# Two rations of filler products for TensorE inside one step of a scan loop

## The chip, the core and the metric

The kernel runs on one core of one Trainium2 chip. A core has five engines that run side by side, each through its own queue: TensorE (PE in the profile, with its weight loads as PEld), VectorE (DVE), ScalarE (ACT), GpSimd (POOL) and SyncE (SP), which here only issues DMAs. The metric is device time in microseconds (us), the median of several runs; smaller is better.

## What is computed

Two layers are applied to an input `x` of 4 batches, 512 channels and 64 x 64 = 4096 positions, in float32. Cut to what matters:

```python
# layer 0: x = x + mamba_layer(group_norm(x)); the 512 channels are 4 chunks of 128
xn  = layer_norm(group_norm(x))
xz  = chunk @ in_proj_w.T                 # 2 x 256 columns: xi and z
xc  = silu(causal_conv4(xi))
dt, Bs, Cs = split(xc @ x_proj_w.T)       # 8, 16 and 16 columns
dt  = softplus(dt @ dt_proj_w.T + dt_proj_b)
h_t = exp(dt_t * A) * h_(t-1) + (dt_t * x_t) * B_t      # 256 x 16 states, 4096 times
y_t = sum_over_states(h_t * C_t) + xc * D
ym  = (y * silu(z)) @ out_proj_w.T + skip * chunk
x   = x + layer_norm(ym) @ proj_w.T + proj_b
# layer 1: x = x + linear_attention(group_norm(x)), 8 heads of 64
q, k = relu(x @ w_q.T), relu(x @ w_k.T)
kq   = k.T @ q, summed over all 4096 positions of a batch
out  = (v @ kq) / kq.sum() @ w_out.T + b_out
```

Layer 1 of a batch can only start when layer 0 of that batch is done, since its group norm and `kq` need all positions.

## The kernel before, in words

**Steps and slots.** Layer 0 is cut into 128 steps: 4 batches, 8 tiles of 512 positions each, 4 chunks of 128 channels (`steps`, in this order). A step is cut into `SLOTS` = 16 slots. A slot makes two scans of 128 x 512 (L741, DVE), the two decays `dA` that they read (L715, ACT, written to three PSUM banks, three scans ahead), and one product `bx` of 128 x 1024 (L723, POOL, two slots ahead). Every second slot closes four scans of one group of states: DVE multiplies them by `c_all` (L761), POOL their last quarter (L753), and TensorE sums over the states into `y` (`fold_states`, 16 short matmuls). So even slots hold one DVE operation more than odd ones.

**Work with a fixed slot.** The inner function `after()`, called at the end of each slot, also issues what the step needs at fixed places: `time_banks` in slot 2, the two softplus in slot 3, `out_proj` of the step before in slot 4, the convolution and gate inputs of the step after next (`front`: `pc`, `pz`) in slots 3 and 5 to 9, its `mixers` (`pd`) in slots 12 to 15 and 0, 1. `take_y` (L780) copies a finished `y` out of PSUM on ACT in slots 8 and 0.

**Filler.** All other work is written as generators that issue a little and then yield. They stand in four lists: `ahead` (the norm of the next tile), `late` (`leave`: the second layer norm, the projection `pp`, the residual add, the statistics of layer 1), `rest` (`attention` of a finished batch: `pq` and `pk`, then the small `pm`, `pob`, and the output `pr`) and `light` (statistics of the next batch). A piece of `pq`, `pp` or `pr` is two products; a bank is filled by two such pieces, with `yield "more"` between them.

**The credit.** `mm()` counts every matmul in units of one 128 x 512 float32 product: bf16 ones count a quarter, ones of which several run side by side a share. At the end of each slot the credit grows by a ration and shrinks by what the slot issued; it never exceeds 2.6. Then each list gets one turn: `ahead` always, `late` and `rest` only while the credit is positive (or for a piece that uses no TensorE, or for the second half of a bank if nothing large was issued in this turn). `limit` and `room` bound how many PSUM banks filler may hold (1 in slots 1 to 5, else 2), `later(n, ...)` puts an eviction `n` slots after its matmuls (`soon()`: 2 in slots 5 to 11, else 1), and `TILES` = 3 bounds the 1 MB tiles in SBUF.

```python
limit[0] = 1 if 0 < s < 6 else 2
credit = min(credit + 3.5 - (work["mm"] - seen), 2.6)
busy = False
for queue in (ahead, late, rest):
    kind = queue[0][1] if queue else None
    if queue is ahead or kind == "free" or credit > 0 or kind == "more" and not busy:
```

**The order is fixed at build time.** All of this is Python that runs when the program is built. On the chip each engine gets a fixed list of instructions; nothing is decided by time.

**After the last slot** what stands in the lists is issued without credit, banks or due times:

```python
add_to(late, leave(B - 1, NT - 1))
while late or rest:
    one(late) or one(rest)
```

The attention of the last batch can only be here, since its layer 0 ends with the last slot. `rest` is a first-in first-out list: an attention of an earlier batch that isn't finished comes first.

Of the kernel before, what the change touches and what calls it, by code (L numbers as in the profile page):

```python
# [24 lines left out]
def kernel(  # L25
# [100 lines left out]
    work = {"mm": 0.0}  # L126
# [486 lines left out]
    def time_banks(f, nm):  # L613

        f["pt"] = [work_bank(f"pt_{nm}_{e}", 0) for e in range(NH)]
        for e in range(NH):
            r = slice(e * LANE, (e + 1) * LANE)
            mm(f["pt"][e], w_dt[r, :], f["dtr"][r, :], start=True, stop=True, abreast=NH)

    def time_steps(f, nm):  # L620
        for e in range(NH):
            nc.scalar.activation(  # L622
                f["both"][:, 0, e, :], f["pt"][e], AF.Softplus, bias=dtb[:, e : e + 1]
            )

    def to_rows(f, v, nm):

        both = f["both"]
        if v:
            nc.gpsimd.tensor_tensor(f["both"][:, 1], f["both"][:, 0], f["xz"][:, 0], ALU.mult)  # L630
        d_rows = dram.tile([P, NH, T], F32, tag=f"d_rows{v}", name=f"d_rows{v}_{nm}")
        f["d_rows", v] = d_rows
        later(1, lambda: nc.sync.dma_start(d_rows, both[:, v]))

    def spread(f, e, nm, part):

        if part == 0:
            f["d_all", e] = wk.tile([P, 2, NJ, T], F32, tag="d_all", name=f"d_all_{nm}_{e}")
        v, half = divmod(part, 2)
        src = f["d_rows", v].rearrange("(j i) e t -> i e j t", i=BLK)[:, e]  # L640
        for k in range(half * KS // 2, (half + 1) * KS // 2):
            nc.sync.dma_start(f["d_all", e][k * BLK : (k + 1) * BLK, v], src)
# [136 lines left out]
    def take_y(f, n, e):  # L779
        nc.scalar.copy(f["xz"][:, 0, e, :], ys.pop((n, e)))  # L780

    def gate(f, e):
        nc.gpsimd.tensor_tensor(  # L783
            f["xz"][:, 1, e, :], f["xz"][:, 1, e, :], f["xz"][:, 0, e, :], ALU.mult
        )

    def out_proj(f, xn, c, nm):
        po = f["po"] = work_bank(f"po_{nm}", 0)
        diagonal(po, skd, xn[:, c, NTAP - 1 : NTAP - 1 + T])
        for e in range(NH):  # L790
            mm(po, w_op[:, e, :], f["xz"][:, 1, e, :], start=False, stop=(e == NH - 1))

    def with_skip(f, xn, c):
        nc.scalar.copy(xn[:, c, NTAP - 1 : NTAP - 1 + T], f["po"])
# [239 lines left out]
    def leave(b, t):  # L1034
        if t == 0:
            stats1[b] = shifted_stats(b)
            x1s[b] = [
                dram.tile([P, NC, T], F32, tag="x1", name=f"x1_{b}_{i}", bufs=3 * NT)
                for i in range(NT)
            ]  # L1040
        ym = xn[b, t][:, :, NTAP - 1 : NTAP - 1 + T]
        yield from projected(ym, stats1[b], x1s[b][t], b, t)
        if t == NT - 1:
            add_to(rest, attention(b, x1s[b], stats1[b]))
# [5 lines left out]
    def silu(n):  # L1050
        xz = fs[n]["xz"].rearrange("p i e t -> p (i e) t")
        nc.scalar.activation(xz[:, : 2 * NH - 1], xz[:, : 2 * NH - 1], AF.Silu)  # L1052
        nc.scalar.activation(xz[:, 2 * NH - 1], fs[n]["pz"], AF.Silu)
# [3 lines left out]
    def add_to(queue, pieces):  # L1057
        queue.append([pieces, None])
# [3 lines left out]
    def one(queue, may=ANYWHERE):  # L1062

        while queue:
            if queue[0][1] not in (None, "wait", "more", "free") and queue[0][1] not in may:
                return False
            queue[0][1] = next(queue[0][0], queue)
            if queue[0][1] is not queue:  # L1070
                return queue[0][1] != "wait"
            queue.pop(0)
        return False
# [26 lines left out]
    with tc.manual_schedule():  # L1100
        credit, seen, mix, held[0], held_x[0] = 0.0, work["mm"], iter(()), 0, 0
        for n, (b, t, c) in enumerate(steps):
# [10 lines left out]
            for s in range(SLOTS):  # L1113
                def after():
                    nonlocal credit, seen
                    now[0] = n * SLOTS + s
                    for what in [w for at, w in due if at <= now[0]]:
                        what()
                    due[:] = [d for d in due if d[0] > now[0]]
                    if s == 0 and before is not None:  # L1120
                        take_y(before, n - 1, 1)
                    if s == SLOTS // 2:
                        take_y(f, n, 0)
                    if s < 2:
                        next(last_mix, None)
                    if s < 4:
                        spread(f, 1, nm, s)
                    if s == 1 and before is not None:
                        gate(before, 1)
                    if s == 2 and nxt is not None:  # L1130
                        time_banks(nxt, names[n + 1])
                    if s == 3 and nxt is not None:
                        nc.scalar.preload_act_table_set("softplus")
                        time_steps(nxt, names[n + 1])
                        nc.scalar.preload_act_table_set("natural_log_exp_and_others")
                    if s == 6 and before is not None:
                        pb_, pt_, pc_ = steps[n - 1]
                        with_skip(before, xn[pb_, pt_], pc_)
                        if pc_ == NC - 1:
                            add_to(late, leave(pb_, pt_))  # L1140
                    if s in (3, 5, 6, 7, 8, 9):
                        next(front, None)
                    if s == 4 and nxt is not None:
                        to_rows(nxt, 0, names[n + 1])
                        to_rows(nxt, 1, names[n + 1])
                    if s == 4 and before is not None:
                        pb_, pt_, pc_ = steps[n - 1]
                        out_proj(before, xn[pb_, pt_], pc_, names[n - 1])
                    if s == 9:
                        gate(f, 0)  # L1150
                    if 8 <= s < 12 and nxt is not None:
                        spread(nxt, 0, names[n + 1], s - 8)
                    if s == 10 and n + 2 < N:
                        silu(n + 2)
                        nc.scalar.preload_act_table_set("natural_log_exp_and_others")
                    if s >= 12:
                        next(mix, None)
                    may = [
                        what for k, what in ((0, "wide"), (1, "one ahead"), (2, "two ahead"))
                        if any(a - 2 * k <= s <= a - k for a in AWAY) or (k == 2 and s == SLOTS - 1)  # L1160
                    ]
                    if light and light[0][1] == "wait" or s in AWAY and not any(
                        q and q[0][1] == "wide" for q in (ahead, late)
                    ):
                        one(light)

                    limit[0] = 1 if 0 < s < 6 else 2
                    credit = min(credit + 3.5 - (work["mm"] - seen), 2.6)
                    busy = False
                    for queue in (ahead, late, rest):  # L1170
                        kind = queue[0][1] if queue else None
                        if queue is ahead or kind == "free" or credit > 0 or kind == "more" and not busy:
                            start = work["mm"]
                            one(queue, ANYWHERE if queue is ahead and (c, s) > (1, 4) else may)
                            credit -= work["mm"] - start
                            busy = busy or work["mm"] - start > 1
                    seen = work["mm"]

                slot(n * SLOTS + s, N * SLOTS, after)
            fs[n - 1].clear() if n else None  # L1180
        product(N * SLOTS - 1)
# [64 lines left out]
```

## Time and profile before

| | |
|---|---|
| Median of 3 runs | 7841.29 us (7840.99 to 7841.53) |
| The profiled execution | 7841.65 us, span 7839.9 us |
| Busy in the span | DVE 88%, POOL 88%, PE 82%, ACT 70% |
| First and last scan start | 121.4 and 7362.8 us |
| After the last scan's end (7364.0 us) | 475.9 us |

The span runs from the first to the last instruction. The rest of the profiled execution's time, 1.75 us, lies around it. In the page "busy" is the time in which an engine works on something; for PE it is not a measure of its peak. The span has two parts that must be read apart: the scan loop from 121 to 7364 us, and a tail in which DVE and POOL have nothing to do. Inside the loop the 4096 scans of L741 are a clock: two are one slot, 32 are one step.

### The profile page before, as it was taken

How to read it: one execution, taken by the hardware profiler on the slowest of the kernel's cores; microseconds unless marked ns; L12 is line 12 of the kernel's file. 1: busy time of each engine (PE TensorE's matmuls, PEld its weight loads, DVE VectorE, ACT ScalarE, POOL GpSimd, SP SyncE). 2: the span in 40 equal slices, each digit the busy share in tenths (PEclk: the TensorE clock that was granted, in tenths of full speed). 3: DMA queues.
4: the chain of work that ended last, by engine and by line, in shares of the span. 5: the costliest groups of instructions: out<-in, count | busy, mean ns of one | idle time of the engine just before them, and what ended most of it. 6: DMA issues, size and time to landing. Idle time of an engine off the chain costs nothing.

```text
span 7839.9 us, 90362 instructions
## 1 busy us (share of the span) xinstructions
PE 6444.6 (82%) x24837; PEld 2113.0 (27%) x24880; DVE 6904.3 (88%) x5650; ACT 5457.0 (70%) x8329; POOL 6904.2 (88%) x4649
## 2 busy tenths in 40 slices
PE   5676777677788888898788888898788888988599
PEld 1121211111223222332222223332122232322144
DVE  5999999999999999999999999999999999999500
ACT  4667777777777777777777777777777777777421
POOL 4999999999999999999999999999999999999500
PEclk7788878888899999998899999999899999999799
DMA  5676666666666666776766666677666666577302
GB/s 163 164 172 165 160 152 162 158 161 166 173 171 171 154 168 166 183 192 172 178 161 173 172 165 162 169 188 181 165 162 167 160 167 156 146 211 182 98 33 91
DMA packets 829183, 1265.86 MB, mean 161 GB/s; under 512 B 183912, under 2 KB 317560, under 8 KB 816384
## 3 DMA queue, kind: packets, MB, share of 16 engines
q1 hardware_dynamic: 804736, 1222.32, 61.2%
q0 software_dynamic: 16896, 33.56, 2.5%
q10 hardware_dynamic: 7040, 4.20, 0.2%
q8 instruction: 195, 3.19, 0.2%
q14 instruction: 316, 2.59, 0.1%
HBM read 1052.78 MB, written 206.57 MB: 161 GB/s over the span
## 4 chain that ended last, share of the span: by engine, by line
DVE 33%; PE 31%; ACT 11%; DMA 8%; issue 7%; POOL 6%; SPq 3%; POOLq 0%; DVEq 0%; ACTq 0%
DVE h L741 21%; DVE h L761 10%; PE y L124 6%; PE pc L124 6%; PE pq L124 5%; POOL bx L723 4%; ACT dA L715 4%; DMA d_all<-d_rows 3%; PE pr L124 3%; PE po L124 3%; PE pp L124 2%; SPq L690 2%; DMA c_sb<-c_rows 2%; PE c_all L124 1%; DMA b_all<-b_rows 1%
## 5 line engine op out<-in xcount | busy, mean ns | idle before, releaser
L723 POOL TENSOR_TENSOR bx<-d_all,b_all 128x1024 f32<-128x1024 f32 x2048 | 4829.5, 2369 | 184.7 <-DVE h L741 164.6
L741 DVE TENSOR_TENSOR_SCAN h<-dA,st,bx 128x512 f32<-128x512 f32 x3584 | 4360.0, 1269 | 317.0 <-ACT dA L715 132.8
L715 ACT ACTIVATE dA<-d_all,a_t 128x512 f32<-128x512 f32 x4096 | 2758.2, 687 | 1491.7 <-DVE h L741 1435.2
L761 DVE TENSOR_TENSOR h<-h,c_all 128x1536 f32<-128x1536 f32 x1024 | 1772.4, 1731 | 0.1
L753 POOL TENSOR_TENSOR h<-h,c_sb 128x512 f32<-128x512 f32 x1024 | 1301.4, 1271 | 108.2 <-DMA c_sb<-c_rows 21.8
L124 PE MATMUL y<-h,fold 128*32 128x512 f32 x8192 | 1271.8, 697 | 30.9 <-POOL h L753 27.3
L124 PE MATMUL c_all<-parts,sel 128*128 128x384 bf16 x1024 | 368.4, 360 | 1077.4 <-DVE h L761 1075.7
L124 PE MATMUL pc<-xn,w_cv 128*128 128x512 f32 x2048 | 1045.0, 644 | 120.8 <-DVE xn L414 63.3
L124 PE MATMUL pq<-w_qk,xa 128*128 128x512 f32 x2048 | 967.8, 606 | 7.5 <-issue 5.0
L741 DVE TENSOR_TENSOR_SCAN h<-dA,bx 128x512 f32<-128x512 f32 x512 | 590.6, 1206 | 80.7 <-ACT dA L715 57.9
L124 PEld LDWEIGHTS <-sel 128*128 128x128 bf16 x1280 | 127.3, 100 | 1733.2 <-DVE h L761 1537.4
L124 PEld LDWEIGHTS pc<-xn,w_cv 128*128 128x128 f32 x2048 | 388.9, 201 | 740.7 <-issue 417.7
L124 PEld LDWEIGHTS pq<-w_qk,xa 128*128 128x128 f32 x2048 | 397.7, 196 | 446.8 <-issue 428.2
L124 PE MATMUL pr<-xb,m 128*128 128x512 f32 x1024 | 477.8, 605 | 5.5 <-ACT res L982 2.8
L124 PE MATMUL pp<-xn,w_pr 128*128 128x512 f32 x1024 | 478.0, 597 | 3.8 <-DVE xn L414 3.8
L124 PE MATMUL y<-xz,dg 32*32 32x512 f32 x2048 | 358.9, 778 | 0.0
L124 PEld LDWEIGHTS y<-h,fold 128*32 128x32 f32 x8192 | 170.5, 114 | 619.6 <-issue 377.1
L783 POOL TENSOR_TENSOR xz<-xz 128x512 f32<-128x512 f32 x256 | 325.9, 1273 | 8.9 <-ACT xz L780 8.3
L834 ACT ACTIVATE kq<-pq 128x512 f32<-128x512 f32 x256 | 150.6, 588 | 260.0 <-PE pq L124 259.0
L630 POOL TENSOR_TENSOR dt<-dt,xz 128x1024 f32<-128x1024 f32 x128 | 302.5, 2363 | 27.8 <-ACT dt L622 27.8
L124 PE MATMUL pd<-xz,w_xp 128*128 128x512 f32 x512 | 309.1, 734 | 5.2 <-ACT xz L1052 5.2
L124 PE MATMUL pz<-xn,w_z 128*128 128x512 f32 x512 | 273.2, 625 | 9.9 <-ACT xz L609 8.5
(178 smaller groups left out, 5927.6 us busy)
## 6 DMA issues: line engine op xcount, KB each, us to landing
d_all<-d_rows SPq DMA_DIRECT2D x2048, 256.0 KB, 4.4
b_all<-b_rows SPq DMA_DIRECT2D x4096, 64.0 KB, 2.4
d_rows<-dt SPq DMA_DIRECT2D x256, 512.0 KB, 3.0
c_sb<-c_rows SPq DMA_DIRECT2D x4096, 16.0 KB, 3.6
xs<-in_x_dram SPq DMA_DIRECT2D x32, 1024.0 KB, 7.5
xn<-in_x_dram SPq DMA_DIRECT2D x32, 1024.0 KB, 8.8
xr<-in_x_dram POOLq DMA_DIRECT2D x32, 1024.0 KB, 10.0
x<-xr SPq DMA_DIRECT2D x32, 1024.0 KB, 4.2
```

Of the source, the lines that this page charges most:

```text
L124: nc.tensor.matmul(out_, lhsT, rhs, **how)
L630: nc.gpsimd.tensor_tensor(f["both"][:, 1], f["both"][:, 0], f["xz"][:, 0], ALU.mult)
L690: nc.sync.dma_start(dst[k * BLK : (k + 1) * BLK, :], rows_[q * KS + k, :].partition_broadcast(BLK))
L715: nc.scalar.activation(dAs[k], fs[n]["d_all", e][:, 0, j, :], AF.Exp, scale=a_t[:, e, j, q : q + 1])
L723: nc.gpsimd.tensor_tensor(bxs[g], fs[n]["d_all", e][:, 1, jj * 2 : jj * 2 + 2, :], bc(b_all[g // JJ], 2), ALU.mult)
L741: nc.vector.tensor_tensor_scan(h[:, j, :], dAs.pop(2 * g + i), bxs[g][:, i, :], 0.0 if t == 0 else st[:, c, e, q, j : j + 1], ALU.mult, AL ...
L753: nc.gpsimd.tensor_tensor(h[:, :, CUT:], h[:, :, CUT:], bc(c_sb.pop(g // JJ), NJ), ALU.mult)
L761: nc.vector.tensor_tensor(own, own, bc(c_all.pop(g // JJ), NJ), ALU.mult)
L783: nc.gpsimd.tensor_tensor(f["xz"][:, 1, e, :], f["xz"][:, 1, e, :], f["xz"][:, 0, e, :], ALU.mult)
L834: nc.scalar.activation(qk[i], pq, AF.Relu)
```

## The change

One line of `after()` is different: the ration that a slot adds to the credit.

```diff
                     limit[0] = 1 if 0 < s < 6 else 2
-                    credit = min(credit + 3.5 - (work["mm"] - seen), 2.6)
+                    credit = min(credit + (2.5 if 2 <= s < 10 else 4.5) - (work["mm"] - seen), 2.6)
                     busy = False
                     for queue in (ahead, late, rest):
```

Slots 2 to 9 of each step add 2.5 products in place of 3.5, slots 10 to 15 and 0 and 1 add 4.5. The sum over a step is 56 both times, and the cap of 2.6 and everything else stay.

## The prediction, as put on record before the changed kernel ran

> **What bounds the kernel now.** I read the busy table and the 40 slices of the page first. DVE and POOL are at 9 tenths until slice 37 and then at 0 while PE is at 8 or 9: a loop in which DVE and POOL are full, and a tail that belongs to PE.
>
> ```profile
> PE 6444.6 (82%) x24837; PEld 2113.0 (27%) x24880; DVE 6904.3 (88%) x5650; ACT 5457.0 (70%) x8329; POOL 6904.2 (88%) x4649
> ...
> PE   5676777677788888898788888898788888988599
> ...
> DVE  5999999999999999999999999999999999999500
> ```
>
> Then sums by window, cut where the scan count says that eight steps end: two windows of eight steps without attention, then two with it, then the tail.
>
> ```profile
> 999.00:1441.00 442.00, 321.08 (x1188) 86.22 (x1188) 423.24 (x328) 322.67 (x491) 429.58 (x288) 0.81 0.66 158
> 1441.00:1883.00 442.00, 318.00 (x1188) 85.61 (x1188) 423.17 (x327) 322.90 (x491) 429.62 (x288) 0.82 0.66 158
> 2334.00:2795.00 461.00, 403.94 (x1670) 137.49 (x1673) 437.92 (x366) 345.67 (x534) 430.99 (x288) 0.95 0.67 170
> 2795.00:3255.00 460.00, 403.72 (x1656) 141.05 (x1657) 428.46 (x344) 342.74 (x528) 433.03 (x294) 0.93 0.65 161
> ```
>
> The columns are PE, PEld, DVE, ACT and POOL, busy us and count. A step takes 442 / 8 = 55.2 us without attention, of which POOL works 429.6 / 8 = 53.7: its floor. With attention it takes 57.6, POOL working 53.9. So attention costs some 2.4 us a step, nearly all of it waiting. Next the waits of DVE from 2334 to 3255 us (16 steps), and the chain of waits over the tail.
>
> ```profile
> DVE h L741 <- ACT dA L715: 16.2, 18, 3.4
> DVE h L741 <- PE y L124: 11.1, 11, 2.3
> DVE h L741 <- ACT kq L834: 8.3, 3, 3.0
> ```
>
> ```profile
> 7389.88 15.71 PE pp L124 x32
> ...
> 7673.26 7.40 PE pq L124 x18
> 7681.44 3.61 PE pq L124 x8
> 7685.78 0.71 PE pk L124 x16
> 7689.36 20.05 PE pm L124 x40
> 7709.41 11.23 PE pob L124 x64
> 7722.82 113.10 PE pr L124 x256
> ```
>
> In the loop late PE results stop ACT, and through it the decays and DVE. In the tail PE alone counts, and one attention stands there: its `pr` rows are 256 instructions, two for each of 8 x 4 x 4 = 128 products.
>
> **What the Trainium skill says.** "PSUM — Partial Sum Buffer", section Engine vs sequencer instructions: the queues of ScalarE, VectorE and GpSimd are strictly first-in first-out, and matmuls complete in program order. The trace agrees: DVE waited 8.3 us above for an eviction of `kq`, which has nothing to do with scans. "SBUF — State Buffer", section Who interferes with whom: a DVE operation with at most one SBUF input, outside the two-port modes, doesn't contend with GpSimd. The scan and L761 each have one operand in PSUM, and the scan's time is even here (1217 to 1297 ns), so moving filler shouldn't stretch DVE's or POOL's own operations. "Perfetto Trace Analysis", section Identifying the Most-Contended Engine: matmul busy time is a poor measure of how full TensorE is. I therefore count products.
>
> **The change, part by part.** No operation is added or removed; pieces move between slots, and possibly out of the loop. The credit rule is plain arithmetic on product counts, so where each piece falls can be counted from the code for both rations. Means per attention step (steps 40 to 59 before and after):
>
> - Slots 2 to 9, all products: 29.0 before, 22.3 after. Of `rest` 6.3 before, 1.2 after. Slots 4 to 9 alone, 21.6 to 15.8.
> - Slots 10 to 15, 0, 1: 21.8 before, 23.9 after. Of `rest` 10.1 before, 10.7 after.
> - Whole step: 50.8 before, 46.3 after.
>
> The sum of the rations is 56 both times, but a turn of `rest` issues one piece of about two products, and credit above 2.6 is lost. In slots 10 to 1 `rest` already ran nearly every turn, so 4.5 there buys little; the 2.5 in slots 2 to 9 is eaten by fixed work. Throughput of filler falls by about 4.6 products a step, and attention no longer keeps pace. Before, the attentions of batches 0, 1 and 2 end at step 62 slot 15, 94 slot 15 and 125 slot 9. After, the list is never empty from step 35 on, and at the loop's end 5734.3 - 5502.0 = 232.3 products of batch 2's attention are left.
>
> *The tail.* 232.3 is: 2 + 1 + 4.25 for what remains of the 24th of 32 position blocks, 8 x 9.5 for eight whole ones, 1 for the last `pk`, 4 + 16 for `pm`, 128 for `pr`, and `pob`, small in products. Their duration is read from the same pieces of batch 3 in the tail of before. A block starts every (7673.26 - 7440.84) / 29 = 8.014 us, and the last starts at 7676.85 (PE's rows in order of time); so the 25th starts at 7676.85 - 7 x 8.014 = 7620.8. `pr` ends at 7722.82 + 113.10 = 7835.9. That is 215.1 us. The rest of the 24th block is 7.25 products of 8.014 / 9.5 = 0.84 us: 6.1. Together 221.
>
> Can the backlog hide in a gap? PE stands idle today from the end of `pp` (7405.6) to the first full `pq` (7427.2), mostly for the residual DMA and statistics on ACT. The backlog can use some 6 us of it; the next block's norm is behind the statistics on ACT (done at 7421.9) and needs two evictions (0.6 each) and 0.8 more, so PE waits to about 7424. In exchange a new joint opens between the two attentions: the last eviction (0.7), the load of the first tile behind the last stores on SP (7.6 us to landing), and a norm of 0.8, some 10 us. These cancel to about +1. Tail: +222 us, bounds 210 and 232.
>
> *The loop.* Steps 35 to 127 take 7364.0 - 2045.2 = 5318.8 us before: 84 at about 57.6, 9 without attention at about 54.4. After, all 93 carry attention. By slot (two scans each), DVE's idle time a step in steps 36 to 61 is 0.73 us in slot 5, 0.28 in 6, 1.07 in 8, 0.19 in 10; in steps 4 to 34 it is 0.39, 0.01, 0.29, 0.01. PE is hardly idle from slot 5 to 9 and still has the 5.5 products of slot 4 before it. With 15.8 products in slots 4 to 9, fewer than the 18.2 of steps 4 to 29, I expect these four slots to fall to the smaller values: -1.5. Against it, slots 12 to 15 go from 12.0 to 13.4 products, with evictions one slot later; their length is 4.24 + 2.66 + 4.03 + 2.53 = 13.5 us, and at 0.84 the 13.4 fill 11.3 of it. A heavy slot 12 (5.1) may delay ACT and `take_y` in slot 0. No row shows this; it lies between 0 and the 1.1 by which the early slots suffered. I take +0.3. A step then takes 57.6 - 1.5 + 0.3 = 56.4 us; 93 x 56.4 = 5245, so -74. Bounds: 55.6 (only POOL's floor and the old idle) gives -148, 57.0 gives -18. Steps 0 to 34 hold the same 34 products a step in the stretch 4 to 29, only later in the step, and stand at 55.2 against POOL's 53.7: 0, bounds -8 and +5. The fixed order of `bx`, scans and their DMAs stays; DMAs of `rest` and `late` (tile loads, the residual add, stores) move a few slots with their pieces, with 35% of the DMA time free. What is late next in the loop is POOL itself.
>
> *The sum.* 7841.65 + 222 - 74 = 7990 against the profiled execution, which lies 0.4 us above the median. The tail and the loop's steps are the only terms.
>
> **The rivals.** First, *the waits don't go*: attention keeps its price of 2.4 us a step because eviction work on ACT causes it, or slots 12 to 1 suffer as 4 to 9 did. At 57.6 the loop takes 5357, +38, and the total is 8102. If instead the price follows the product count, (46.3 - 34.3) / (50.8 - 34.3) x 2.4 = 1.75 makes 56.95 a step, -22: 8042. For it: heavy pieces now crowd before `take_y` in slot 0. Against: PE still has gaps in slots 10 to 2 (waits of `c_all` for L761). Second, *the loop runs almost at POOL's floor*: 55.2 a step, as without attention, gives 5134, -185, total 7879. For it: step 2 of a tile with 43.9 products and no attention takes 55.3. Against: DVE has 1.2 us a step more to do (434 - 423 over 8). Third, the other side: *the loop pays the whole tail*. One mechanism: evening out the load ends every stall in slots 5 to 8 and also those that exist without attention. It decides from (5318.8 - 222) / 93 = 54.8 us a step, below the 55.2 of steps without attention; at 54.6 the time would be 7823. Against it: POOL's 53.7 to 53.9 leaves then 1 us of idle where 1.5 was the best. That the change does nothing is excluded: the backlog is in the instruction lists.
>
> **How the numbers follow.** Forecast (55.6 to 57.0 a step): 0.66, 7990. Waits stay or follow the product count fully (above 57.0): 0.21, 8050 to 8102. Near the floor (54.9 to 55.6): 0.10, around 7879. Not slower: 0.03. The range takes the forecast's own bounds, 7841.65 + 210 - 148 = 7904 and 7841.65 + 232 - 18 = 8056, widened to 7895 and 8075 for the two neighbours; that leaves 0.2 out. A measurement here can tell 0.2%, 16 us, from no change: slower 0.95, same 0.02, faster 0.03.
>
> **What would show it.** After the change the last scan should end about 7290 us, and the tail be near 700 us long with two sets of `pr` (512 instructions) and two of `pm`. Steps with attention should take about 56.4 us, DVE's waits in slots 5, 6 and 8 should shrink, and none should be left free of attention after step 35. The prediction is wrong if steps still take 57.6 (then it is too low), or if the loop ends before 7142 (then it isn't slower at all).

## The result, and the profile after

The changed kernel takes 8041.17 us (median of 4 runs, 8037.68 to 8047.91). Against the kernel before, 7841.14 us in the same comparison, the ratio is 1.0257 (95% interval 1.0245 to 1.0269): 200 us slower. The profiled execution took 8047.91 us, its span is 8046.2 us. The page's busy table and two rows of its 40 slices, as for the kernel before:

```profile
PE 6526.8 (81%) x24828; PEld 2125.7 (26%) x24880; DVE 6901.2 (86%) x5650; ACT 5466.9 (68%) x8329; POOL 6899.0 (86%) x4649
...
PE   5677777777788888888888888888888888888999
...
DVE  5999999999999999998999999999999999996000
```

Busy times are those of before within 0.2%, PE's apart (+82 us); what grew is the stretch at the end in which DVE has nothing to do. The scan row of the changed kernel (least, median and longest ns, first and last start) says where the loop ends:

```profile
L741 DVE TENSOR_TENSOR_SCAN h<-dA,st,bx x3584: 1212/1258/1287, 334.9 to 7374.2; 128x512 f32<-128x512 f32 x200
```

The last scan started at 7362.8 us before and starts at 7374.2 now. So the loop is 11 us longer, and what lies behind its last scan grew from 475.9 to 670.7 us: +195. The changed kernel's chain of waits over that tail (start, us, what):

```profile
7396.05 14.02 PE pp L124 x32
...
7489.31 19.13 PE pm L124 x40
7508.44 8.58 PE pob L124 x64
7519.19 112.48 PE pr L124 x256
...
7635.59 12.26 PE pq L124 x24
...
7897.14 20.23 PE pm L124 x40
7917.37 11.08 PE pob L124 x64
7930.61 111.57 PE pr L124 x256
```

Two attentions stand in the tail where one stood: `pm`, `pob` and `pr` come twice. The leftover of batch 2 runs from the end of `pp` (7410.1) to the end of its `pr` (7519.19 + 112.48 = 7631.7): 221.6 us. Windows of eight steps each with attention, steps 40 to 47 and 48 to 55, then the tail (start and end, length, busy us and count of PE, PEld, DVE, ACT and POOL, then the granted TensorE clock, the DMA share and GB/s):

```profile
2341.00:2800.00 459.00, 381.33 (x1547) 122.33 (x1550) 437.91 (x369) 333.13 (x505) 430.10 (x287) 0.93 0.65 166
2800.00:3252.00 452.00, 375.24 (x1510) 121.11 (x1510) 426.32 (x336) 339.88 (x522) 428.22 (x287) 0.92 0.63 159
7375.00:8046.00 671.00, 640.60 (x2189) 298.69 (x2207) 26.05 (x65) 144.51 (x230) 13.56 (x26) 0.97 0.21 74
```

PE does less in the loop, 381 and 375 us for eight steps against 404 before, but the steps are hardly shorter.

### The profile page after: what moved, and what is told of

The parts are those of the page before. It is cut to its first block, busy times and chain, and to the rows that moved or that the text cites. A ratio compares the mean times of both kernels' runs of the same rounds, so it can differ in the third digit from the quotient of the medians.

```text
span 8046.2 us, 90394 instructions
## 1 busy us (share of the span) xinstructions
PE 6526.8 (81%) x24828; PEld 2125.7 (26%) x24880; DVE 6901.2 (86%) x5650; ACT 5466.9 (68%) x8329; POOL 6899.0 (86%) x4649
## 4 chain that ended last, share of the span: by engine, by line
DVE 36%; PE 28%; ACT 9%; issue 8%; DMA 8%; POOL 6%; SPq 3%; DVEq 0%; POOLq 0%; ACTq 0%
DVE h L741 24%; DVE h L761 11%; PE y L124 6%; PE pq L124 6%; POOL bx L723 4%; PE pr L124 4%; PE pp L124 3%; DMA d_all<-d_rows 3%; ACT dA L715 3%; PE pc L124 3%; SPq L690 2%; DMA c_sb<-c_rows 2%; PE pd L124 2%; DMA b_all<-b_rows 1%; PE po L124 1%
## 5 line engine op out<-in xcount | busy, mean ns | idle before, releaser
L124 PE MATMUL y<-h,fold 128*32 128x512 f32 x8192 | 1274.1, 698 | 46.7 <-POOL h L753 45.8
L124 PE MATMUL pc<-xn,w_cv 128*128 128x512 f32 x2048 | 1064.0, 655 | 124.0 <-ACT dt L622 47.3
L124 PE MATMUL pp<-xn,w_pr 128*128 128x512 f32 x1024 | 484.1, 607 | 16.8 <-ACT xr L514 10.8
L124 PE MATMUL y<-xz,dg 32*32 32x512 f32 x2048 | 382.0, 825 | 0.0
L630 POOL TENSOR_TENSOR dt<-dt,xz 128x1024 f32<-128x1024 f32 x128 | 301.8, 2358 | 47.9 <-ACT dt L622 47.6
L841 DVE TENSOR_TENSOR kq<-pk,kq 128x256 f32<-128x256 f32 x124 | 50.9, 410 | 336.4 <-PE pk L124 336.4
```

What stands on the lines that cost most here:

```text
L124: nc.tensor.matmul(out_, lhsT, rhs, **how)
L841: nc.vector.tensor_tensor(kq, pk, kq, ALU.add)
```

## The experiments

The two questions were what the leftover costs by itself, and why the loop with fewer products in it did not get shorter. "Left" is what the instruction lists leave of batch 2's attention at the loop's end. Loop and tail are of the profiled execution: the start of the last scan, and span less that. "Step" is the mean length of the 76 steps in which both the kernel before and this one have attention in the loop (36 to 61, 68 to 93, 100 to 123), from the times of the scans, 32 to a step. The two parts of a step are lengths: they hold DVE's own work as well as its waits.

| rations (slots 2 to 9 / 10 to 1) | left | last scan | tail | step, and its slots 2 to 9 + 10 to 1 | median us | ratio to before, 95% interval |
|---|---|---|---|---|---|---|
| 3.5 / 3.5, before | 0 | 7362.8 | 477 | 57.63 = 29.68 + 27.94 | 7841 | |
| 2.5 / 4.5, the change | 232 | 7374.2 | 672 | 57.41 = 28.50 + 28.91 | 8041 | 1.0257, 1.0245 to 1.0269 |
| 3.0 / 3.0 | 210 | 7288.2 | 655 | 56.50 = 29.03 + 27.47 | 7951 | 1.0145, 1.0130 to 1.0160 |
| 3.5 / 4.5 | 0 | 7406.1 | 477 | 58.27 = 30.10 + 28.16 | 7887 | 1.0063, 1.0046 to 1.0079 |
| 4.5 / 2.5 | 0 | 7533.4 | 477 | 59.41 = 31.48 + 27.93 | 8008 | 1.0214, 1.0199 to 1.0229 |
| 2.5 / 4.5, second halves at once | 76 | 7404.9 | 531 | 57.74 = 28.44 + 29.30 | 7933 | 1.0119, 1.0102 to 1.0135 |
| 3.0 / 4.5 | 0 | 7372.3 | 472 | 57.62 = 28.69 + 28.94 | 7847 | 1.0010, 1.0004 to 1.0017 |
| 3.25 / 3.25 | 20 | 7304.3 | 482 | 56.85 = 28.75 + 28.10 | 7788 | 0.9937, 0.9922 to 0.9952 |
| 3.22 / 3.22 | 22 | 7278.2 | 484 | 56.76 = 28.92 + 27.83 | 7762 | 0.9902, 0.9885 to 0.9918 |

**An even ration of 3.0: nearly the same leftover without the uneven pattern.**

```diff
-                    credit = min(credit + 3.5 - (work["mm"] - seen), 2.6)
+                    credit = min(credit + (3.0) - (work["mm"] - seen), 2.6)
```

> A ration of 3.0 in all 16 slots: an even pattern with too little throughput. 210.3 products of attention are left at the loop's end, nearly as many as the 232.3 of the changed kernel. Theory A: tail = 476 + 6.5 blocks x 8.0 + 151 - 27 (gaps that the backlog fills in the changed kernel) = 652, loop about 7375, total about 8025. Rival B (the uneven ration itself costs): without it the loop falls below 7340 and the total below 7995. Rival C (each product in the loop costs about 0.14 us): loop 7335.

The tail came out at 653 us from the last scan's end, one us off theory A's sum. The loop is 75 us shorter than before, not 11 longer, so theory A's loop (7375) was missed by 87. The tail is priced by what is left over, whatever the pattern; and a thinner even ration does shorten the loop. Eight steps of this kernel with attention, DVE third and POOL fifth:

```profile
2323.00:2778.00 455.00, 379.07 (x1545) 124.32 (x1544) 435.85 (x361) 331.97 (x502) 428.95 (x287) 0.94 0.65 165
```

A step issues 46.7 products here and 46.3 in the changed kernel (both counted in the lists, steps 40 to 59), yet takes 56.5 us against 57.4. Of the 86 us by which the two loops differ, 68 lie in the 93 steps with attention, and 18 in steps 0 to 34, which end at 2035.4 us here and at 2053.3 in the changed kernel. Rival C's size (7335) was too small, rival B's threshold (loop below 7340) was met.

**The change's rations with the throughput nearly restored.** In slots 10 to 1 the second half of a bank may follow its first half in the same slot:

```diff
+                    if not 2 <= s < 10 and rest and rest[0][1] == "more" and credit > 0:
+                        start = work["mm"]
+                        one(rest, may)
+                        credit -= work["mm"] - start
                     seen = work["mm"]
```

> The changed kernel's rations; in slots 10 to 1 the second half of a bank of `rest` may follow in the same slot where credit is left. The late slots stay as full as in the changed kernel, but only 76 products (part of the last `pr`) are left at the loop's end in place of 232.3. Theory A (what is left over is what costs the 200 us): tail = 476 + 76 x 0.88 - 29 for gaps filled = 514, loop 7370 to 7410, total 7885 to 7925. Rival B (the late-heavy pattern costs in the loop and the backlog is cheap): total 7980 or more.

Left over are 76 products in place of 232, and the tail shrinks from 672 to 531 us. The loop is at the upper end of what theory A gave; the total of 7933 is 8 us above its band, since the tail is 16 longer than the 514 of its sum. The pattern itself doesn't make the 200 us; but the 156 products that now go into the late slots make the loop 31 us longer. A stronger form, a second turn for `rest` in each of these slots that was to leave nothing over, gave no time: its order of instructions deadlocks.

**The halves of the change, and the mirror.** The ration is written as the change writes it, with 3.5 and 4.5, 3.0 and 4.5, and 4.5 and 2.5.

> 3.5 products in slots 2 to 9 as before, 4.5 in slots 10 to 1: the half of the change that adds. By the instruction lists no attention is left at the loop's end, and each ends a step or two earlier than before. Theory A (the tail pays for what is left over, and in the loop a step with attention costs about 2.3 us whatever the pattern): tail 476 us as before, six steps fewer with attention, loop about 7350, total 7825 to 7835. Rival B (heavier slots 10 to 1 are what made the loop of the changed kernel lose its gain): loop longer than before, total 7860 or more.

> 3.0 in slots 2 to 9, 4.5 in slots 10 to 1; nothing is left at the loop's end. Against the run with 3.5 and 4.5 only the early ration is thinner. Theory D (early filler costs, the late ration of 4.5 costs as well): loop 30 to 60 us below that run's 7407, so 7345 to 7380, total 7820 to 7860. Rival (the late ration costs nothing, only early filler does): loop below 7330, total below 7810.

> 4.5 in slots 2 to 9 and 2.5 in slots 10 to 1: the mirror image. Nothing is left for the tail. Theory A: tail 476, loop within 25 us of before, total 7815 to 7866. Rival B (an uneven ration costs by itself): total 7950 or more. My own recorded step (filler in slots 4 to 9 is what makes attention steps long): loop 40 to 100 us longer than before, total 7880 to 7940.

All three finish every attention in the loop and keep the old tail (472 to 477 us). The higher late ration alone makes the loop 43 us longer, where theory A had it shorter: a miss for A, a hit for B. Taking the early ration from 3.5 to 3.0 wins 34 of them back, inside theory D's band. The mirror is the worst loop of all, 171 us longer, beyond even what my recorded step gave. Its total also meets rival B's threshold, so the time alone doesn't say whether early filler or unevenness costs; the waits do. Its waits of DVE over the attention steps:

```profile
DVE h L741 <- PE y L124: 235.6, 161, 3.7
DVE h L741 <- ACT dA L715: 124.4, 114, 6.9
```

and of ACT:

```profile
ACT xz L780 <- PE y L124: 146.9, 100, 3.4
```

L780 is `take_y`, 57.2 us before (1930 to 7364). With 32.2 products in slots 2 to 9 (29.0 before) TensorE reaches the last fold of `y` late, ACT stands in front of it with the decays queued behind, and slot 9 is 3.9 us long in place of 2.7. So filler in the early slots does cost, as the prediction said; what it missed is how much late filler costs.

DVE's waits by slot (that of the instruction that waits, means over the same 76 steps) separate the two. In slots 8 and 10 they follow the early ration in all nine kernels of the table: 2.78 us a step at 4.5, 1.20 and 1.16 at 3.5, 0.83 and 0.79 at 3.25 and 3.22, 0.72 and 0.44 at 3.0, 0.29 and 0.25 at 2.5. In slots 5, 6 and 11 to 2 together they go with the late one: 2.65 to 3.17 us in the four kernels with 4.5, 1.76 to 2.27 in the five with less. The change takes the first group from 1.20 to 0.29 and the second from 2.27 to 3.17: it gains 0.9 us and pays 0.9.

**Where the late cost sits.** DVE's waits in the changed kernel, from 1930 to 7376 us:

```profile
DVE h L741 <- ACT dA L715: 164.3, 127, 4.7
DVE h L741 <- PE y L124: 91.7, 89, 2.2
DVE kq L841 <- PE pk L124: 26.5, 19, 2.5
```

against the kernel before, from 1930 to 7364:

```profile
DVE h L741 <- ACT dA L715: 121.8, 106, 6.6
DVE h L741 <- PE y L124: 83.4, 86, 3.0
DVE kq L841 <- PE pk L124: 20.4, 21, 2.9
```

The waits for a decay grew by 42 us. By slots (steps 36 to 123) most of that is slot 5: 0.77 us a step before, 1.13 after, 32 us in these 88 steps. Slot 5 counts as an early slot in the table, so this part of the late cost stands in the column of slots 2 to 9. So it does where the late ration alone was raised: of the 0.64 us by which a step grew there, 0.42 are in that column. Ahead of slot 5 ACT has the softplus of slot 3 with its table loads. Evictions of `pq` and `pr` that ACT does in slots 0 and 1 rose from 47 to 70 in these steps, and the last softplus starts 16.8 us after its step does, 16.0 before. Attention is not alone in this: `late` obeys the same credit, and ACT's waits for the `pp` of `leave` nearly doubled. Before and after, from 1930 to 7300 us:

```profile
ACT xr L514 <- PE pp L124: 48.1, 61, 2.5
ACT xr L514 <- PE pp L124: 89.0, 71, 3.2
```

Of the 89 us, 25.0 lie in slot 0 and 25.4 in slot 4 (by time), where it was 1.2 and 0. POOL feels it as well: the product behind the softplus (L630) waits 47.6 us in the page where it waited 27.8.

The column of slots 10 to 1 grew by 0.97 us, but 0.39 of it is no wait. The pass of `leave`'s layer norm on DVE (L414, 2.27 us) may be issued in slots 3 and 10 alone; in 13 of the 18 times that it falls into the 76 steps it moved from slot 3 to slot 10, and the column of slots 2 to 9 lost the same 0.39. DVE's idle time went from 2.49 to 1.90 us a step in slots 2 to 9 and from 1.17 to 1.70 in the others: in sum it stayed the same within 0.1.

In one more run only the additions of `pk` on DVE that stem from slot 12 were put off:

```diff
-            return later(soon(), lambda: add(pk, v == 0))
+            return later(2 if now[0] is not None and now[0] % SLOTS == 12 else soon(), lambda: add(pk, v == 0))
```

> The changed kernel, with the addition of `pk` to `kq` on DVE that stems from slot 12 put two slots later in place of one; 232.3 products are left as in the changed kernel. In the changed kernel DVE waits 0.39 us a step in slot 13 for `pk`. Theory E (this wait is part of what the late ration costs): 93 steps x 0.2 to 0.4, so 20 to 36 us shorter, total 8000 to 8022. Rival (the wait is covered, since POOL is the bound in these slots): within 10 us of 8041.

It took 7998.65 us (1.0204, 1.0188 to 1.0219), just below theory E's band, the loop 47 us shorter, the tail the same within 2 us; waits for `pk` fell to

```profile
DVE kq L841 <- PE pk L124: 6.8, 7, 1.4
```

which is 20 of the 47; the waits for decays fell too, 164 to 135, and ACT's for `pp`, 89 to 69. (The 0.39 us a step of the expectation holds for steps 36 to 61; over steps 36 to 123 it is 0.19.) The same edit in two other kernels:

> The kernel before (3.5 in all slots) with the same edit as the run that moved the addition of `pk` from slot 12 by one slot. Theory E (the edit helps only where the late ration crowds slots 12 and 13): DVE waits only some 0.05 us a step for `pk` in slot 13 here, so 0 to 10 us shorter, total 7828 to 7841. Rival F (late additions cost the same whatever the ration, so that the gain had nothing to do with the change): 25 us or more shorter, total below 7815.

> 3.0 in slots 2 to 9, 4.5 in slots 10 to 1, with the same edit. Nothing is left at the loop's end. Five `pk` pieces stand in slot 12 here against twelve in the changed kernel. Theory E: 5/12 of the 42 us, so 10 to 20 us below that ration without the edit (7847), total 7827 to 7837. Rival (the gain of the edit was a shift of everything after it): no change, 7840 to 7855.

With 3.5 it gave 7825.08 (0.9985, 0.9978 to 0.9991), somewhat more than theory E, far less than rival F; with 3.0 and 4.5 it gave 7844.96 (1.0008, 0.9999 to 1.0016), against 7846.62 without: nothing, a miss for theory E. There the edit had moved 2 additions from slot 13 to 14 in the 88 steps, where the expectation counted five. With 3.5 it moved 9, about as many as the 10 that stem from slot 12 in the changed kernel, and gained 12 us in place of 42. So the edit has no price per addition that could be carried over. Putting an eviction off also holds its bank longer and shifts every later piece, and part of the 47 us may be that.

**Is slot 4 the culprit among the early ones?**

```diff
-                        if queue is ahead or kind == "free" or credit > 0 or kind == "more" and not busy:
+                        if queue is ahead or kind == "free" or (credit > 0 or kind == "more" and not busy) and not (queue is rest and s in (4,)):
```

> The kernel before (3.5 in all slots), but `rest` gets no turn in slot 4, the fullest one: 4.4 products there in place of 5.5, the pieces going to slots 5 to 8; nothing is left at the loop's end. Theory G (the pile-up in slot 4 is what makes DVE wait in slots 5 and 8): attention steps 0.4 to 0.8 us shorter, total 7775 to 7810. Rival (the sum of products in slots 2 to 9, the same 29, is what counts): within 12 us of 7838.

7845.52 us, 1.0003 (0.9994 to 1.0012): no change. DVE's wait in slot 8 was halved (0.92 to 0.45 us a step) and turned up in slot 10 (0.26 to 0.76), where it waits for PE's `y`. The pile moved with its pieces: as the rival had it, the same sum in slots 2 to 9 gave the same time.

**A version better than both.**

> A ration of 3.25 in all slots: 20 products are left at the loop's end. Theory D (an even and thinner ration shortens the loop as 3.0 did, by 75 us, in proportion to the products that leave a step; the leftover hides in the tail's gap of 21 us): loop 7320 to 7345, tail 470 to 480, total 7795 to 7825, faster than before. Rival (the loop of the 3.0 run was short only because of the 210 products that it didn't do): loop 7355 to 7365, total about 7840.

> A ration of 3.22 in all slots; 22 products are left at the loop's end, the same amount within 2 as with 3.25, but the pieces fall in other slots. Theory D (what counts is that attention just fits into its 93 steps with an even ration): total within 12 us of the 7788 of 3.25. Rival (3.25 hit a lucky order): 7810 or more.

> A ration of 3.22 with the `pk` additions of slot 12 one slot later. As the same edit gained 42 us with the changed ration, 12 us with 3.5 and nothing with 3.0 and 4.5, it is expected to move pieces about rather than to have a price of its own: total 7750 to 7775, within 12 us of 7762.

3.25 gave 7787.89 us, below its band's lower end by 7, and 3.22 gave 7762.31, better than its own band: 75 us or 1.0% less than the kernel before in the same comparison. Both spread each attention over nearly all the steps that it has, and leave 20 or 22 products of `pr` that run mostly in the gap after `pp` (tails of 482 and 484 us, 477 before). With the late addition too, 3.22 gave 7774.66 (0.9914, 0.9898 to 0.9930), at the upper end of its band and no better. Two lists that differ by 0.03 in the ration are 26 us apart, and I have no step-by-step account of that difference. One of DVE's waits in the 3.22 kernel, from 1930 to 7280 us:

```profile
DVE h L741 <- PE y L124: 53.8, 76, 3.8
```

Against the 83.4 us of the kernel before, 30 us went from the waits for `y`.

## Why the prediction was right, and where it wasn't

The forecast was 7990 us, slower by 149; measured were 8041, slower by 200, inside the range. The tail did what the prediction said, 27 us less of it. The loop did not: it was to gain 74 us and lost 11. By its steps:

- **The backlog**: 232.3 products left of batch 2's attention, with the 25th block as the first whole one. The list of TensorE instructions after the loop is that: `pr` has 512 instructions in the tail. Right.
- **Its duration**: 221 us, measured 221.6 from the end of `pp` to the end of `pr`. The two are not quite the same thing: 3.9 us of the 221.6 are a stop that is shown below, and two products ran earlier, between the matmuls of `leave`. Like for like it is about 219. Right.
- **The gaps**: "These cancel to about +1" is wrong by 28 us; the tail grew by 195, not 222. TensorE before, first work after the end of `pp` at 7405.6:

```profile
7422.61 0.59 PE L124 MATMUL pm_b<-mv_b,grp 128*128 128x4 f32 x2 [17.04 <-POOL mv_b L575]
```

  TensorE after, its rows in order of time behind the last `pp`:

```profile
7409.98 0.69 PE L124 MATMUL pk<-kq 128*64 128x64 f32 x16
7410.60 0.39 PE L124 MATMUL pq<-bqk,sel 128*128 128x512 bf16 x1
7410.83 3.60 PE L124 MATMUL pq<-w_qk,xa 128*128 128x512 f32 x8
...
7422.49 3.60 PE L124 MATMUL pq<-w_qk,xa 128*128 128x512 f32 x8
7429.96 1.12 PE L124 MATMUL pk<-kq 128*64 128x64 f32 x16 [3.87 <-ACT kq L834]
```

  The tile of the 25th block needn't wait for the statistics on ACT: its norm ran from 7369.9 us on, still in the loop. PE stood still for 3.9 us only, where I had 12. At the joint between the two attentions I had 10 us and the chain above shows 3.9 (7631.7 to 7635.6). So the 21.6 us gap of before (7405.6 to 7427.2, the first full `pq`) was nearly all filled. Another 7 us came from the last `leave`, which ran from the last scan's end to the end of `pp` in 34.7 us, not 41.6.
- **The early slots**: slots 5, 6, 8 and 10 were to lose 1.5 us of DVE's waits a step. Slots 8 and 10 lost 0.9, about as forecast; slots 5 and 6 rose from 1.19 to 1.46 us a step (76 steps), where 0.6 less was forecast. Their waits go with the late ration and not with filler in slots 4 to 9: in the mirror, with more early filler, they stand at 1.04. The table's 28.50 - 29.68 = -1.2 looks like a near hit, but 0.39 of it is the moved layer norm. The waits that do follow the early ration fell by 0.9 in all.
- **The late slots**: +0.3, "between 0 and the 1.1 by which the early slots suffered". The waits that go with the late ration, those of slots 5 and 6 among them, rose by 0.9. I had priced the late slots by TensorE's capacity, 13.4 products in 13.5 us of slots, and feared for `take_y` in slot 0; ACT's waits there rose only from 6.0 to 13.5 us in 88 steps. What grew instead are ACT's waits for other evictions, those of `pp` in slots 0 and 4 above all, and DVE's waits for `pk`. That these make the 0.9 is read from the waits; of them only the additions of `pk` were moved by a run of their own.
- **Steps 0 to 34**: taken as 0 with bounds -8 and +5; they grew by 8, just outside.
- **The loop in all**: -74 forecast, +11 measured, 8 of it in steps 0 to 34 and 3 in the 93 others. A step was to take 56.4 us and took 57.4, close to the 57.6 that was named as the sign of too low a forecast. The step of the prediction that failed is this price of an attention step: it set a gain of 1.5 against a cost of 0.3, and the waits show about 0.9 against 0.9. It is the second of the ways listed under "the waits don't go", "slots 12 to 1 suffer as 4 to 9 did", that came true. The first, an unavoidable price of attention, did not: at 3.0 the step is 1.1 us shorter, at 3.22 0.9. The rival of product counts named 8042 and so hit the total within 1 us, but by luck: its loop was to be 22 us shorter, and its tail was the 222 of the forecast. It has the right sign for even rations and fails for uneven ones.

One thing that was to stay did stay: the moved filler did not stretch the scans, 1212 to 1287 ns after and 1217 to 1297 before.

So two errors of opposite sign, +85 in the loop and -27 in the tail, left the profiled execution 58 us above the forecast and the median 51. That the range held the result is in part due to this: with the loop as measured and the tail as forecast, the time would have been 7841.65 + 222 + 11 = 8075 us, its upper end. Both costs fit the strict queues that the prediction took from the Trainium skill's "PSUM — Partial Sum Buffer" (Engine vs sequencer instructions): the trace shows ACT standing 146.9 us for `y` in the mirror and 89.0 us for `pp` in the changed kernel, with decays behind these instructions in its queue.

What stays open: how the late 0.9 us splits between the evictions of `leave`, those of attention and DVE's waits for `pk`, and why 3.22 beats 3.25 by 26 us. No run moved the late evictions on ACT alone, or gave `late` and `rest` different rations.

## What to carry to other kernels

A ration that keeps its sum can still lower the throughput, when work comes in pieces and unused credit is cut off: count what is left at the end of the loop before asking what the loop gains. Work that fell out of a loop whose bound lies elsewhere costs its full price in the tail, here 0.95 us a product (221.6 / 232.3) less the gaps that it fills, where in the loop it had cost 0.3 to 0.4 (57.63 - 56.50 for 50.8 - 46.7 products at 3.0, 57.63 - 56.76 for 50.8 - 48.5 at 3.22). A slot here was full not when TensorE was, but when an in-order engine that evicts its results had to wait: the best of the rations tried was even and let each attention take nearly all the steps that it has. And when two halves of a loop are compared by length, ask first whether work moved across the border.

## What I had not expected of the hardware

In the last `leave` TensorE ran faster after the change. Its granted clock was 1.00 from 7375 to 7396 us, where it was 0.61 from 7364 to 7390 us before, and the 32 `pp` instructions took 14.02 us in place of 15.71. Two things differ: pieces of `pq` stand among its short matmuls now, and TensorE was busier in the last slots of the loop. The kernel with 3.0 has the second alone. Its last 19 us of the loop and the chain of short matmuls in `leave`, behind the same two stretches of the kernel before (columns as above, the clock third from the end):

```profile
7345.00:7364.00 19.00, 9.98 (x37) 1.57 (x37) 16.99 (x14) 5.53 (x8) 12.76 (x9) 0.59 0.31 117
7364.00:7390.00 26.00, 14.74 (x27) 2.94 (x28) 4.05 (x3) 6.87 (x11) 2.72 (x3) 0.61 0.00 0
7270.00:7289.00 19.00, 16.92 (x76) 5.69 (x74) 18.57 (x16) 8.33 (x13) 14.68 (x11) 0.95 0.18 63
7289.50:7310.00 20.50, 12.34 (x55) 2.97 (x51) 4.37 (x3) 9.32 (x15) 2.73 (x3) 0.99 0.00 0
```

So the pieces between are not needed for the full clock in that chain. In these two kernels it went with how busy TensorE had been just ahead of it, 16.9 of 19 us against 10.0. That is no rule yet: with 3.0 and 4.5 TensorE was busy for 16.4 of the last 19 us, and the clock in the chain was 0.71. Nor do the pieces explain the faster `pp`: the run that put off the additions of `pk` has the same pieces there, and its `pp` took 15.8 us.
